# A graph network's edge sort and message stage: places from pairwise comparisons, halves of 9 and 9 edge tiles, seven target classes

## The chip, the cores and the metric

The kernel runs on one core of a Trainium2 chip, in one launch. The metric is device time in microseconds. An execution is timed as a whole; one further execution is recorded by the hardware profiler, and everything said about where the time goes comes from that one.

## What is computed

The graph has 3,125 nodes with 256 features and 50,000 edges with 16 features each. Sources are random; targets are drawn with a square law, and edges come ordered by target. One layer of message passing, then three graph convolutions over the same edges, each block behind a layer norm and a ReLU:

```python
h = jnp.maximum(_layernorm(x, axis=-1), 0.0)
# block 1
msg_input = jnp.concatenate([h[src], h[dst], edge_features], axis=-1)
messages = jax.nn.relu(msg_input @ mW1 + mb1) @ mW2 + mb2
aggregated = jax.ops.segment_sum(messages, src, num_segments=3125)
u = jax.nn.relu(jnp.concatenate([h, aggregated], -1) @ uW1 + ub1)
x = x + h + u @ uW2 + ub2
# block 2, three layers, gelu between them
h = jnp.maximum(_layernorm(x, axis=-1), 0.0)
# layer: y = h @ W; out = segment_sum(y[src] * dis[src] * dis[dst], dst) + b
x = x + gcn(gelu(gcn(gelu(gcn(h)))))
```

The hidden width is 512; `dis` is one over the root of a node's count of incoming edges, itself included.

## The kernel before

**Layout.** Node n belongs to node tile t = n mod 25, and its row in the tile is n div 25, so there are 25 node tiles (`NT`) of 125 rows (`NP`). The edges lie on chip as 128 partitions by 391 columns (`SCOLS`); a column is 128 edges.

**Stage 1, the sort (to about 565 us).** Each edge is given a place in a table in HBM, `rows_d`, sorted by the node tile of its source and, inside that, by a class of its target. There are two tables, for two halves of the edges: the first 240 columns (`SPLIT`) and the other 151. In the first a node tile has room for 11 edge tiles of 128 edges, in the second for 7 (`KT`). A row holds 20 numbers (features, target, row of the source in its tile, column of the target in the adjacency matrix).

The place of an edge is the number of edges of the same key before it. The key is 5 x source tile + target class, 125 values, one for each partition. `load_keys` broadcasts the keys of up to 24 columns from HBM (`bk_d`) to all partitions; `sort_chunk` (L330 to L392) compares them with the partition's number (L336, `eq`), runs a prefix sum over four columns at a time (L345, `cum`), adds what came before (`carry`, L351), keeps it where the key matches (L348, `q`), and lets a matmul with ones collapse the partitions to one place per edge (L354, `p_pos`). Some small VectorE steps turn places into row numbers (L358 to L376); ACT copies build the rows (`pay`, L386 to L389). In the first half each column is then scattered by an indirect DMA that GpSimd issues (L170, 128 rows of 80 bytes). The second half's rows wait on chip in `pay1` and `place1`. `fills` first writes empty rows to both tables.

Between the chunks of columns the program places other work, by position in the program: layer norm statistics (L151), h = relu(norm(x)) (`norm`), the tables `tabA` and `tabB` (L427), which hold h times the source's and the target's part of `mW1`, and the counting of incoming edges by one-hots (`count_edges`: ACT, L470 and L473, and a matmul, L475). The stores of these tables and of h transposed (`hT`, L422) go out on SyncE's queue (SP), which also issues the loads of edge features (`ea_st`) and of the broadcast keys.

**Stage 2, the messages (565 to 1850).** For each half q and node tile t, for each edge tile k of that node tile: GpSimd gathers the targets' rows of `tabB` (L725, `gb`, five buffers); PE makes the features' and the source's part (L730, L732, `p_x`); VectorE adds them (L733), ACT and VectorE make the ReLU in two pieces (L735, L736, `m`); PE sums over the edges of a source by a one-hot (L746, `p_sum`). Beside the edge tiles of one node tile run the adjacency counts of the one before: `counts` (L674) compares the targets' columns with an iota for a class of 626 columns (L681, `od`), once for each pair of class and edge tile that can meet (`REACH`), and PE multiplies it with the source's one-hot in two pieces of 313 columns (L683, `p_A`, one buffer of two banks); `counted` moves each class to the matrix A (L697 by ACT in the first half, L701 added by VectorE in the second). In the first half, the scatters of the second half's rows are put between the gathers, spread over the edge tiles of the first 24 node tiles. In the second half the node update (`nd`, L539 to L574) runs beside the edge tiles too, two node tiles late.

A test of the counts against `REACH` sets a flag, and a message stage that goes edge column by edge column stands behind it for inputs that do not fit.

**Stage 3, three graph layers (1850 to 2431).** PE multiplies A with the node products (L1004) in 7 blocks of 448 columns.

PE, VectorE (DVE), ScalarE (ACT), GpSimd (POOL) and SP each work through their instructions in program order. What stands ahead in an engine's or a queue's order holds up what is behind it.

## Time and profile before

| | us |
|---|---|
| median of three runs (2421.38 to 2439.94) | 2425.44 |
| the profiled execution | 2433.28 |
| its span, first to last instruction | 2431.6 |
| busy: PE, PEld, DVE, ACT, POOL | 1948.0, 1570.6, 1561.4, 1010.5, 858.9 |
| first scatter, last place computed, first edge tile | 72.5, 550, 565 |
| second half of the messages begins | 1275 |

Engines are named PE (TensorE matmul), PEld (weight load), DVE (VectorE), ACT (ScalarE), POOL (GpSimd), SP (SyncE). In a row of a group, the line and the engine come first, then what is written and read with the shapes (partitions x elements), the count, and after the bar the busy time in us and the mean time of one in ns; then the idle time of the engine just before these instructions and what ended most of it. The slices show busy time in tenths in forty equal parts of the span; PEclk is the granted clock of TensorE in tenths. A chain of waits is the work that ended last, followed back from its end; "issue" is time in which an engine waited for nothing that the profile shows, "remote" and "another core or an unknown queue" an event whose source the profile does not know.

### The profile page before, as it was taken

Reading aid. Unit: us, or ns where it says so; the run is one execution under the profiler, and the core shown is the slowest. Engines: PE = TensorE matmul, PEld = TensorE weight load, DVE = VectorE, ACT = ScalarE, POOL = GpSimd, SP = SyncE. Lnnn points to the kernel's source line nnn. Section 1 sums busy time; section 2 is a strip of 40 time slices with the busy share of each in tenths; the row PEclk is TensorE's granted clock in tenths of the full one; section 3 lists DMA queues with packets and bytes.
Section 4 is the critical chain, followed back from the end, with each engine's and each line's share of the span. In section 5 each row is a group of like instructions: output and inputs, shape, how many; then the busy total and the mean of one; then the engine's idle time right before and its main releaser. Section 6 shows DMA issues by size and latency. Waiting matters only on the chain.

```text
span 2431.6 us, 30795 instructions
## 1 busy us (share of the span) xinstructions
PE 1948.0 (80%) x10314; PEld 1570.6 (65%) x10314; DVE 1561.4 (64%) x3618; ACT 1010.5 (42%) x2070; POOL 858.9 (35%) x895
## 2 busy tenths in 40 slices
PE   3224554675888888888889999999996999999993
PEld 3223232354665666665667888888885898998992
DVE  4636343595877888887879999999983323223221
ACT  0415443452444545454444444444433544434440
POOL 0656656304666666666653332333210000000000
PEclk9999666776999899999989999999997999999995
DMA  7102343325544444444444444444432000000003
GB/s 223 43 6 82 101 148 86 101 102 160 152 135 135 130 140 140 136 140 131 136 135 143 142 142 136 144 141 142 142 86 77 22 1 1 1 1 1 1 1 107
DMA packets 117792, 242.64 MB, mean 100 GB/s; under 512 B 19790, under 2 KB 65348, under 8 KB 117491
## 3 DMA queue, kind: packets, MB, share of 16 engines
q0 software_dynamic: 48512, 122.02, 18.5%
q1 hardware_dynamic: 55996, 103.64, 13.2%
q10 hardware_dynamic: 13108, 14.84, 2.0%
q8 instruction: 85, 1.39, 0.2%
q14 instruction: 91, 0.75, 0.1%
HBM read 193.31 MB, written 47.12 MB: 99 GB/s over the span
## 4 chain that ended last, share of the span: by engine, by line
PE 58%; DVE 12%; issue 7%; another core or an unknown queue 7%; DMA 7%; ACT 5%; POOL 2%; ACTq 1%; SPq 0%; DVEq 0%; POOLq 0%
PE p_o L1004 17%; PE p_A L683 8%; PE p_sum L746 7%; PE p_x L732 7%; PE nd L563 4%; PE p_x L730 3%; DVE gb L733 3%; PE p_g L974 2%; DVE od L681 2%; DVE m L736 2%; PE p_tab L427 2%; PE tr L665 2%; DMA out<-xrow 2%; PE nd L572 2%
## 5 line engine op out<-in xcount | busy, mean ns | idle before, releaser
L725 POOL DMA_INDIRECT gb<-tabB,rows x450 | 454.6, 1010 | 590.0 <-DVE m L736 410.2
L170 POOL DMA_INDIRECT rows_d<-pay,place x391 | 398.1, 1018 | 254.1 <-issue 116.6
L1004 PE MATMUL p_o<-a,g 125*128 125x448 f32 x2100 | 443.1, 370 | 0.0
L1004 PEld LDWEIGHTS p_o<-a,g 125*128 125x128 f32 x2100 | 394.7, 188 | 32.4 <-ACT g L976 0.3
L746 PE MATMUL p_sum<-m,oh 128*125 128x512 f32 x900 | 389.5, 466 | 18.8 <-issue 8.2
L735 ACT ACTIVATE m<-gb 128x512 fp32r<-128x512 f32 x450 | 283.4, 634 | 227.8 <-DVE gb L733 161.3
L683 PE MATMUL p_A<-od,oh_h 128*125 128x313 f16 x1800 | 360.5, 305 | 21.3 <-ACT A L697 11.1
L733 DVE TENSOR_TENSOR gb<-gb,p_x 128x512 f32<-128x512 f32 x450 | 305.0, 678 | 81.3 <-remote 24.7
L732 PE MATMUL p_x<-apc,ohT 125*128 125x512 f32 x900 | 344.5, 430 | 8.9 <-ACT ohT L667 6.7
L736 DVE SCALAR_TENSOR_TENSOR m<-gb,m 128x512 fp32r<-128x512 f32 x450 | 306.4, 684 | 64.7 <-ACT m L735 43.4
L681 DVE TENSOR_SCALAR od<-iota_h,dloc 128x626 f16<-128x626 f16 x900 | 331.6, 397 | 7.9 <-PE p_A L683 6.4
L683 PEld LDWEIGHTS <-oh_h 128*125 128x125 f16 x1800 | 246.8, 140 | 95.4 <-issue 35.0
L998 DVE CAST a<-A 125x448 fp32r<-125x448 uint8 x262 | 102.8, 393 | 273.7 <-PE p_o L1004 273.5
L1000 ACT CAST a<-A 125x448 fp32r<-125x448 uint8 x263 | 148.7, 566 | 240.8 <-PE p_o L1004 240.8
L730 PE MATMUL p_x<-wE,payT 128*128 128x512 f32 x450 | 209.7, 466 | 25.4 <-DVE gb L733 20.7
L746 PEld LDWEIGHTS p_sum<-m,oh 128*125 128x125 f32 x900 | 172.7, 196 | 80.5 <-ACT m L735 17.6
L732 PEld LDWEIGHTS p_x<-apc,ohT 125*128 125x128 f32 x900 | 174.7, 198 | 32.8 <-ACT ohT L667 13.3
L427 PE MATMUL p_tab<-wAB,hT 128*125 128x512 f32 x200 | 126.7, 791 | 73.6 <-issue 46.2
L354 PE MATMUL p_pos<-ones_r,q 128*128 128x2 f32 x391 | 83.0, 323 | 72.4 <-DVE carry L351 40.4
L427 PEld LDWEIGHTS p_tab<-wAB,hT 128*125 128x125 f32 x200 | 48.6, 256 | 134.5 <-issue 104.7
L354 PEld LDWEIGHTS p_pos<-ones_r,q 128*128 128x128 f32 x391 | 72.8, 262 | 86.8 <-issue 42.4
L668 ACT CAST oh_h<-oh 128x375 f16<-128x375 f32 (+1 forms) x125 | 71.2, 569 | 135.8 <-DVE oh L659 121.6
(193 smaller groups left out, 2437.9 us busy)
## 6 DMA issues: line engine op xcount, KB each, us to landing
apc<-tabA SPq DMA_DIRECT2D x50, 500.0 KB
tabA<-a_sb SPq DMA_DIRECT2D x25, 500.0 KB
bk<-bk_d SPq DMA_DIRECT2D x16, 768.0 KB
gb<-tabB,rows POOLq DMA_INDIRECT x450
rows_d<-pay,place POOLq DMA_INDIRECT x391
tabB<-b_sb SPq DMA_DIRECT2D x25, 250.0 KB
R_d<-R SPq DMA_DIRECT2D x25, 250.0 KB
R<-R_d SPq DMA_DIRECT2D x25, 250.0 KB
```

Source lines behind the costliest of these rows:

```text
L170: s = nc.gpsimd.indirect_dma_start(out=rows_d[q], in_=pay, in_offset=None, out_offset=bass.IndirectOffsetOnAxis(ap=place, axis=0))
L427: nc.tensor.matmul(p, hT[:, k, :], wAB[:, s, k, :], start=k == 0, stop=k == 1)
L681: nc.vector.tensor_scalar(od, iota_h, dloc[q, t][:, g, k:k + 1], None, op0=ALU.is_equal)
L683: nc.tensor.matmul(p[:, h_, :HALF], oh_h[q, t][:, k, :], od[:, h_ * HALF:(h_ + 1) * HALF], start=k == lo, stop=k == hi)
L725: gathers[0] = nc.gpsimd.indirect_dma_start(out=gb, out_offset=None, in_=tabB, in_offset=bass.IndirectOffsetOnAxis(ap=row[q, t][:, k, C_DS ...
L730: nc.tensor.matmul(p, payT[q, t][:, k // 2, :], wE[k % 2], start=True, stop=False)
L732: nc.tensor.matmul(p, ohT, apc[q, t][:, s, :], start=False, stop=s == 1)
L733: nc.vector.tensor_add(gb, gb, p)
L735: nc.scalar.activation(m[:, 0, :], gb, AF.Relu)
L736: nc.vector.scalar_tensor_tensor(m[:, 1, :], gb, 0.0, m[:, 0, :].bitcast(F32), op0=ALU.max, op1=ALU.subtract)
L746: nc.tensor.matmul(p_sum[t], oh, m[:, s, :], start=k == 0 and s == 0, stop=k == KT[q] - 1 and s == 1)
L1004: nc.tensor.matmul(po[:, f, :AW], g[:, s, q, f * P:(f + 1) * P], a, start=s == 0 and q == 0, stop=s == NT - 1 and q == 1)
```

## The change

1. **Places.** The broadcast of keys through HBM, the prefix sums over one-hot keys and the carries go. For four columns at a time, `same_bucket` lets PE spread each column's keys over the partitions (a matmul of an identity column with the transposed keys), VectorE compares each edge's key with those of the other 127 of its column and keeps the earlier ones (`same`), and PE sums them. PE also turns the one-hots of the source tile (`eqT`), to look up for each edge how many edges of its key lie in earlier columns (`base`). These come from counts per column, made by one small matmul per column, and one prefix sum over 25 partitions by 7 classes by all columns of the half (`begin_places`).
2. **Halves and chunks.** 195 and 196 columns instead of 240 and 151; room for 9 and 9 edge tiles per node tile instead of 11 and 7. The chunks after which places are written are of 15 and five of 36 columns, then five of 36 and 16, instead of 24 each. `pay` has four buffers instead of three, `ea_st` three instead of two, `hT` three instead of two.
3. **Classes.** Seven target classes of 448 columns instead of five of 626. `od` is made once for an edge tile, over all classes that it can meet (one to four, 448 to 1,792 wide), instead of once for each pair. `p_A` is one bank with two buffers.
4. **Order.** Layer norm and tables run beside the first half's sort only, and all of the counting beside the second's. Of 25 blocks of counting one-hots, 16 are made by VectorE, one instruction a column, and 9 by ACT as before. Fills are four DMAs on SP instead of ten on ACT's queue. The load of x waits for the keys. What prepares the message stage (`wE`, `iota_h`, `first`) moves under the sort; the node weights load when the second message half begins, in `pay1`'s space.
5. Rows of A are now contiguous, so `col()` goes, and the graph layers' row of `dis` is one load.

```diff
-SPLIT = 240
-CH = 24
-KT = (11, 7)
-NG, GT = 5, 5
-REACH = (((0, 2), (1, 4), (3, 6), (5, 8), (6, 10)), ((0, 1), (0, 3), (1, 4), (3, 5), (4, 6)))
+SPLIT = 195
+CHUNKS = [15] + [36] * 5, [36] * 5 + [16]
+KT = (9, 9)
+NG, AW = 7, 448
+REACH = (((0, 1), (0, 2), (1, 4), (2, 5), (3, 6), (4, 7), (5, 8)),) * 2
+CLASSES = [[[g for g in range(NG) if r[g][0] <= k <= r[g][1]] for k in range(n)]
+           for r, n in zip(REACH, KT)]
...
+        def begin_places(q):
...
+            for b in range(NT):
+                nc.vector.tensor_scalar(eq_s[q][:, b, :n], cs_h[:, a:e], float(b), None,
+                                        op0=ALU.is_equal)
...
+                for c in range(m):
+                    nc.tensor.matmul(p[:NT, c * NG:(c + 1) * NG], eq_s[q][:, :, c0 + c - a],
+                                     eq_g[:, :, c0 + c], start=True, stop=True)
+                nc.scalar.copy(by_c[:, c0 - a:c0 - a + m, :],
+                               p[:NT, :m * NG].rearrange("t (c g) -> t c g", g=NG))
...
+            nc.vector.tensor_tensor_scan(cum, ones[:NT, 0:1].to_broadcast([NT, NG * n]), cnt, 0.0,
+                                         op0=ALU.mult, op1=ALU.add)
+            nc.vector.tensor_sub(base[q].rearrange("t g c -> t (g c)"), cum, cnt)
...
-            eq = g1.tile([P, P * CH], BF16, name="eq", bufs=2)
-            nc.vector.tensor_scalar(eq[:, :n], bk[j][:, :n], pid[:, 0:1], None, op0=ALU.is_equal)
...
-                nc.vector.tensor_tensor_scan(cum[:, :m], ones_p[:, 0:1].to_broadcast([P, m]),
-                                             eq[:, a], 0.0, op0=ALU.mult, op1=ALU.add)
...
-                    nc.tensor.matmul(pp[:, c, :], qq[:, c * P:(c + 1) * P], ones_r,
-                                     start=True, stop=True)
+        def same_bucket(q, c, n):
+
+            bc = gps.tile([P, R4, P], F32, name="bc", bufs=2)
+            for j in range(n):
+                i, r = divmod(c + j, P)
+                m = min(P, SCOLS - i * P)
+                nc.tensor.matmul(bc[:, j, :], ident_h[:m, r:r + 1].to_broadcast([m, P]),
+                                 bkT[:m, i, :], start=True, stop=True)
+            t = gps.tile([P, R4, P], F32, name="eqT_ps")
+            for j in range(n):
+                nc.tensor.matmul(t[:NT, j, :], eq_s[q][:, :, c + j - HALVES[q][0]], ident_h, start=True, stop=True)
+            same = g1.tile([P, R4, P], F16, name="same", bufs=3)
+            for j in range(n):
+                nc.vector.scalar_tensor_tensor(same[:, j, :], bc[:, j, :], bkey[:, c + j:c + j + 1],
+                                               tri, op0=ALU.is_equal, op1=ALU.mult)
+            eqT = g1.tile([NT, R4, P], F16, name="eqT", bufs=3)
+            nc.scalar.copy(eqT[:, :n, :], t[:NT, :n, :])
+            return same, eqT
...
+                for j in range(n):
+                    nc.tensor.matmul(pp[:, u + j:u + j + 1], same[:, j, :], ones_h, start=True,
+                                     stop=True)
+                    b = CW + (u + j) * NG
+                    nc.tensor.matmul(pp[:, b:b + NG], eqT[:, j, :],
+                                     base[q][:, :, c0 + u + j - HALVES[q][0]],
+                                     start=True, stop=True)
+                if u + n == w:
+                    placed(q, c0, w, pp)
+                if i >= behind:
+                    beside(i + 1 - behind, len(parts) - behind)
...
         def counts(q, t, g, k):
...
-            od = mp.tile([P, GS], F16, name="od", bufs=4)
-            nc.vector.tensor_scalar(od, iota_h, dloc[q, t][:, g, k:k + 1], None, op0=ALU.is_equal)
-            for h_ in range(2):
-                nc.tensor.matmul(p[:, h_, :HALF], oh_h[q, t][:, k, :],
-                                 od[:, h_ * HALF:(h_ + 1) * HALF],
-                                 start=k == lo, stop=k == hi)
+            if g == own[0]:
+                od = mp.tile([P, iota_h.shape[1]], F16, name="od", bufs=6)
+                n = len(own) * AW
+                nc.vector.tensor_scalar(od[:, :n], iota_h[:, :n], dloc[q, t][:, k:k + 1], None,
+                                        op0=ALU.is_equal)
+                targets[q, t, k] = od
+            b = (g - own[0]) * AW
+            nc.tensor.matmul(p_A[t], oh_h[q, t][:, k, :], targets[q, t, k][:, b:b + AW],
+                             start=k == lo, stop=k == hi)
```

`begin_places` runs once at the start of each half; `same_bucket` is called one group of four columns ahead of the matmuls that use it; `placed` ends a chunk with VectorE steps as before (two more, which pick the class), the row copies and, in the first half, the scatters.

## The prediction

> **What bounds the kernel now.** First the slices of the span, then the busy time by stage, to see which stage has an engine at its limit.
>
> ```profile
> PE 3224554675888888888889999999996999999993
> DVE  4636343595877888887879999999983323223221
> PEclk9999666776999899999989999999997999999995
> ```
>
> ```profile
> 70.00:250.00 180.00, 48.53 (x250) 41.06 (x250) 86.73 (x204) 61.27 (x170) 115.41 (x120) 0.97 0.17 46
> 250.00:450.00 200.00, 109.89 (x422) 60.63 (x422) 89.39 (x155) 80.91 (x214) 113.27 (x116) 0.69 0.38 110
> 450.00:568.00 118.00, 71.80 (x337) 48.82 (x338) 85.69 (x191) 56.91 (x146) 15.83 (x19) 0.69 0.35 113
> 568.00:1275.00 707.00, 600.88 (x2790) 437.43 (x2790) 560.55 (x1201) 341.57 (x617) 446.31 (x426) 0.92 0.48 138
> 1320.00:1820.00 500.00, 498.81 (x3247) 440.62 (x3246) 476.10 (x1209) 206.90 (x408) 145.87 (x154) 1.00 0.46 135
> ```
>
> Columns of the second view: the stretch, its length, busy PE, PEld, DVE, ACT, POOL, granted clock, DMA share, GB/s. Three stages read differently. The sort (to about 565) fills no engine: its busiest, DVE, is at 54% (the first 70 us add 35.6). The first half of the messages (568 to 1275) has PE at 85%, the second (to 1820) PE at 100%. The rest, three graph layers, is PE at 100% and is not touched.
>
> Then the chains of waits of the sort (70 to 560) and of the second message half (1320 to 1820):
>
> ```profile
> by line: another core or an unknown queue 22.5%; issue 19.4%; PE p_tab L427 10.1%; POOL rows_d L170 8.1%; DVE cum L345 7.3%; ACT off L470 5.9%; DMA rows_d<-pay,place 4.8%; DVE q L348 4.7%; ACT oh L473 2.9%; DMA tabB<-b_sb 2.7%; DMA rows<-ro
> ```
>
> ```profile
> by line: PE p_A L683 19.5%; PE nd L563 16.4%; PE p_sum L746 15.3%; PE p_x L732 14.5%; PE nd L550 8.4%; PE nd L572 8.0%; PE p_x L730 7.3%; PE tr L665 3.4%; PE nd L552 2.1%; PE nd L539 2.0%; PE tr L651 1.8%; DVE od L681 0.3%; DVE m L736 0.3%;
> ```
>
> In the sort 41.9% of 490 us, 205 us, is on no engine. The timeline shows a part of it: instructions that wait for nothing start 1.40 us apart while POOL scatters.
>
> ```profile
> 132.44 0.27 DVE L462 TENSOR_SCALAR eq_c<-cs_b 128x391 bf16<-128x391 bf16 x1 [1.07 <-issue]
> 132.88 0.96 POOL L170 DMA_INDIRECT rows_d<-pay,place  x1 [0.30 <-issue]
> 133.84 0.27 DVE L462 TENSOR_SCALAR eq_c<-cs_b 128x391 bf16<-128x391 bf16 x1 [1.13 <-issue]
> ```
>
> Another part is queueing on SP: loads of features and of broadcast keys wait there for buffers, ahead of the tables' stores (hT waits 89.9 us for "remote", ten times). Last the groups that give prices:
>
> ```profile
> L170 POOL DMA_INDIRECT rows_d<-pay,place x391 | 398.1, 1018 | 254.1 <-issue 116.6 <-DVE carry L351 93.3 <-ACT pay L389 19.7
> L681 DVE TENSOR_SCALAR od<-iota_h,dloc 128x626 f16<-128x626 f16 x900 | 331.6, 397 | 7.9 <-PE p_A L683 6.4 <-PE tr L665 1.3
> L345 DVE TENSOR_TENSOR_SCAN cum<-ones_p,eq 128x512 f32<-128x512 f32 x97 | 115.6, 1217 | 6.5 <-remote 4.4 <-issue 1.3 <-DVE cum L345 0.8
> L348 DVE SCALAR_TENSOR_TENSOR q<-cum,carry,eq 128x512 fp32r<-128x512 f32 x97 | 71.5, 737 | 15.6 <-remote 10.9 <-issue 3.0 <-DVE ln_st L151 0.9
> L354 PE MATMUL p_pos<-ones_r,q 128*128 128x2 f32 x391 | 83.0, 323 | 72.4 <-DVE carry L351 40.4 <-DVE q L348 14.5 <-DVE b_sb L436 7.1
> L336 DVE TENSOR_SCALAR eq<-bk,pid 128x3072 bf16<-128x3072 bf16 x16 | 16.2, 1012 | 5.9 <-DMA bk<-bk_d 5.9
> ```
>
> **Sort, what leaves and what comes.** DVE loses scan, q, carry (14.1) and eq: 115.6+71.5+14.1+16.2 = 217 us. It gains 391 comparisons of 128 wide. No row has them: the same operation takes 0.17 us at 24 elements (L360), 0.616 at 384 and 0.737 at 512, so 0.30 by the line between the first two and 0.37 by that between the last two; since successors start some 0.08 us before an end, 0.23 is the low end. I take 0.25, nearer to the short form: 98 us (90 to 145). Place computations are 12 x 11 steps of some 0.2 us for 16 x 8 of 0.1 (now 0.16 to 0.18, overlapped): 13 more; counting one-hots moved from ACT are 256 x 0.10 = 26 (391 wide back to back is 0.174), two scans of 1,365 elements at 1,217/512 ns each 6.5. DVE falls from 297 to about 224.
>
> The Trainium skill ("VectorE: DVE Perf Modes", on the fixed extra latency of each SBUF-source instruction) speaks against many narrow instructions: one wide tile pays the fixed part once, small ones each time. Its formula (N+151)/0.96 gives 290 ns at 128, against 712 at 512 where the row has 737; the comparisons would then be an estimated 114 us, not 98, and the sort 16 us longer at most.
>
> PE loses 83 us (L354) and gains per column two 128-column f16 matmuls, two small ones, and a count that replaces one as large. An f16 matmul of 313 columns takes 0.133 us in the second message half, L475's with 25 columns 0.11 to 0.12 at low clock: 0.10 and 0.07, so 0.34 x 391 = 133 (95 to 200). PE to 568 goes from 259 to 309 and is now the busiest. ACT gains 98 copies of about 0.6 and loses 16 of 25 blocks of L470 and L473 (158 us in all): 42 less. The 17 broadcasts of keys leave SP (12.5 MB). Feature loads get a third buffer, so they no longer hold back the stores there; the fills (four, from 10) go to SP too, behind the first loads and ahead of nothing that is wanted before 70 us. The x load now waits in ACT's queue for the keys (landed at 22.7 us); behind it stand ACT's key copies, which need them anyhow, and DVE's comparison of keys stands behind the first normalisation statistics, which need x.
>
> **Sort, the path.** Scatters run 1.26 us apart (0.96+0.30). The first started at 72.5; x landed at 31.8 and will be later, but no keys go through memory: I keep 70 (60 to 80). POOL then sends 15, waits in its queue (a memset of the next pay, behind ACT's copies) to about 100, and the other 180 take 228: done at 328, which ends nothing but its own rows. ACT's copy of the sixth payload waits for the 36 scatters of the second to land, about 150; layer norm, table copies and eqT copies stand behind it. From there 25 tables at 5.2 us (chain pieces 3.5 at full clock, 7.3 at worst) = 130, beside 21 parts of four columns at 4 x 0.34 = 1.4: 29. The first half ends near 310. The second has no scatters and DVE work of 49+7+26+13+8 = 103; at 0.73, DVE's share in 450 to 568, 141 us: 451. The first edge tile follows in 14 (before, 548 to 565; its preparation moves under the sort): 465, **100 us earlier**. Ends: 400, if PE or DVE keep over 90% in the second half; 565 below.
>
> **Messages, first half (9 tiles for 11).** From the chain of the second half, 22.9 node tiles in 500 us: p_A 19.5% = 4.25 us per node tile, 0.133 each of 32; node update 36.9% = 8.05; the rest 42.3%, 1.32 per edge tile. At full clock before: 11 x 1.32 + 40 x 0.133 = 19.8; after, with 25 matmuls of 448 columns (0.190 each): 9 x 1.32 + 4.75 = 16.6. Measured 28.3, so by PE 28.3 x 16.6/19.8 = 23.7. DVE per node tile, busy 22.4: two edge tiles less, 2.7; `od` from 20 x 0.397 = 7.9 to nine of 448 to 1,792 wide, 9 x 0.24 + 11,200 x 0.25 ns = 5.0 (slope from 626 at 397 to 3,072 at 1,012): about 17. POOL has 17.04 instructions per node tile now (426 in 25) and 9 + 196/24 = 17.2 after: 21.6 us, so it goes from 76% to 91% of the period. That close, I add 0.6: 24.3 x 25 = 608, **99 less** (555 at POOL's pace and little else; 665 at 26.6).
>
> **Messages, second half (9 for 7).** 8.05 + 4.75 + 9 x 1.32 = 24.7 against 21.8: **+72**. It has no slack, PE is at 100%; DVE comes to about 23.5, hidden under it, and would add up to 12 if it led. Node weights (about 2 MB on SP) now load in this half's first node tile, behind the same scatters as its rows; first used two node tiles on, free, 14 us uncovered. p_A's second buffer saves PE 11.1 us of waits (L697), inside the 608. The graph layers keep their 7 blocks, and one load replaces five: 0.
>
> **Sum.** 2433.3 (span 2431.6 and 1.7 around it) - 100 - 99 + 72 = 2306. The profiled run stands 7.8 over the median: **2298**.
>
> **Rivals.**
> - *Gain lost in the sort.* It keeps the old efficiency, busiest engine 54%, so it ends at 309/0.54 = 572, 22 later. For it: the 205 us on no engine are unexplained. Against it: the second half has no scatters and SP lost its queue. Then 2433 + 22 - 27 - 8 = 2420, from 2385 to 2440.
> - *More gain.* The sort ends at 400 (-151) and the first message half runs at POOL's pace (-152): 2433 - 151 - 152 + 72 - 8 = 2194, from 2150 to 2225. Against it: that stage has held 70% of PE's full-clock pace (19.8 of 28.3).
> - *Slower: loss per instruction.* The 205 us belong to the 2,686 instructions of PE, DVE and ACT to 568, 76 ns each. The change makes about 4,350 of them (PE 2,650): 332 us lost, where the rest falls only by some 12 us of work, so the first edge tile comes at about 680: 2433 + 115 - 27 - 8 = 2513. It decides from 56 ns each, where a loss of 244 eats both gains (205 + 27 + 12). For it: the 1.40 us grid holds whatever the instruction is. Against it: the longest of these waits end with SP's stores, which no count explains.
>
> What the Trainium skill says of instruction fetch ("Runtime: NRT & Kernel Launch", Instruction fetch mechanics) counts against the last one: refills come ahead of use and are hidden by the issue rate. By it the loss would not grow with their number; this trace shows 85 and 91 refill packets but not who waited for them.
>
> That the counts exceed a class's reach, so that edges go column by column, is excluded: counted from the inputs, every range holds.
>
> **How the numbers follow.** Forecast (first edge tile at 430 to 520, messages within 40 of their sum): 2225 to 2385, 0.62. More gain 0.14. Gain lost 0.13, most of it within 1% of 2425 (2401 to 2450, about what can be told from no change). Slower 0.11. The range 2190 to 2430 leaves out slower and half of more gain. Faster 0.62 + 0.14 + 0.05 = 0.81, same 0.08, slower 0.11.
>
> **What would show it.** PE and DVE over 70% in the last 130 us before the first gather; that gather at 440 to 490; "issue" and "unknown" under 150 us in the sort's chain; node tiles 24 and 24.7 us apart; POOL over 85% of its pace in the first. Wrong if the sort's second half takes over 200 us, or gathers come to bound PE.

## The result, and the profile after

The changed kernel takes 2515.24 us (median of 4 runs, 2513.37 to 2517.27), the one before 2432.69 (4 runs, 2421.38 to 2440.48). The ratio is 1.0343 [1.0291, 1.0395]: **slower**, where 2298 and faster had been forecast. The profiled execution has a span of 2515.5 us against 2431.6. Cut at the first and the last sum of edge messages (`p_sum`) and at the second half's first gather, the span falls into these stages:

| us | before | after | measured | forecast |
|---|---|---|---|---|
| to the first `p_sum` (sort) | 576.3 | 638.6 | +62 | -100 |
| first message half | 692.9 | 648.8 | -44 | -99 |
| second message half | 545.9 | 624.1 | +78 | +72 |
| the rest | 616.5 | 604.1 | -12 | 0 |

First the slices of the span of the kernel after; each digit is the busy share of a fortieth of it, in tenths, in the last row the granted clock.

```profile
PE   3435546698677787787799999999997999999993
DVE  4323323466566676676689999999995323323221
POOL 1554354100666666666643333333330000000000
PEclk9999678655789898898999999999998999999995
```

The first ten slices, the sort, look no denser than before, and DVE is emptier. Then the busy time by stage (stretch, its length, busy PE, PEld, DVE, ACT, POOL, granted clock, DMA share, GB/s):

```profile
70.00:250.00 180.00, 79.14 (x487) 52.24 (x486) 56.51 (x201) 38.26 (x94) 93.33 (x100) 0.99 0.14 35
250.00:450.00 200.00, 102.05 (x473) 54.73 (x472) 64.57 (x222) 32.73 (x73) 92.91 (x96) 0.74 0.32 91
490.00:617.00 127.00, 120.18 (x989) 97.02 (x987) 87.39 (x393) 50.05 (x107) 0.00 (x0) 0.50 0.01 4
640.00:1285.00 645.00, 492.98 (x2037) 344.99 (x2036) 432.26 (x805) 296.26 (x597) 428.32 (x410) 0.88 0.45 130
1310.00:1900.00 590.00, 588.39 (x3448) 485.68 (x3446) 556.41 (x1304) 263.25 (x543) 208.63 (x215) 1.00 0.49 144
```

Two things stand out. From 70 to 450 PE is busy 48% and DVE 32%: the first half of the sort lasts until about 490 instead of 310. And the second half, 127 us long, has PE at 95% at a granted clock of 0.50. The chain of waits gives no pieces for 65 to 635 of this kernel, so the timeline has to show where the first half's time goes. ACT's row, then PE's, while 36 scatters run from 99 to 144 (start, duration, and in brackets the idle time before and what ended it):

```profile
113.31 0.57 ACT L341 CAST eqT<-eqT_ps 25x512 f16<-25x512 f32 x1 [7.97 <-remote]
139.99 0.57 ACT L341 CAST eqT<-eqT_ps 25x512 f16<-25x512 f32 x1 [26.11 <-remote]
```

```profile
113.93 0.59 PE L335 MATMUL eqT_ps<-ident_h,eq_s 128*25 128x128 f16 x4 [6.34 <-issue]
...
116.61 0.19 PE L409 MATMUL p_pos<-base,eqT 25*128 25x7 f16 x1
140.62 0.58 PE L335 MATMUL eqT_ps<-ident_h,eq_s 128*25 128x128 f16 x4 [23.82 <-issue]
```

The input of ACT's second copy was written by PE at 114.5; the copy starts at 140.0, and PE stands from 116.8 to 140.6. Summed from the instruction records up to the last place, stretches of over 1 us in which PE, ACT and DVE all stand (called the standstill below) make 169 us of the sort here and 114 us before, nearly all of them while scatters are being issued one after the other. Of these, 156 us here and 66 before end with a wait that the profile puts down to "remote", as in ACT's two rows. The groups that the forecast priced:

```profile
L338 DVE SCALAR_TENSOR_TENSOR same<-bc,bkey,tri 128x128 f16<-128x128 f32 x391 | 115.2, 342 | 184.3 <-remote 109.9 <-PE bc L331 59.5 <-PE p_tab L459 7.9
L406 PE MATMUL p_pos<-ones_h,same 128*128 128x1 f16 x391 | 72.9, 187 | 3.3 <-issue 2.8 <-DVE same L338 0.6
L409 PE MATMUL p_pos<-base,eqT 25*128 25x7 f16 x391 | 72.3, 185 | 6.8 <-DVE base L310 6.8
L335 PE MATMUL eqT_ps<-ident_h,eq_s 128*25 128x128 f16 x391 | 61.4, 292 | 69.3 <-issue 50.1 <-ACT eqT L341 18.6
```

The comparisons cost 115.2 us, and the 109.9 us of "remote" ahead of them are the same standstill seen from DVE.

### The profile page after: what moved, and what is told of

Read it like the earlier page. It is cut to its first block, busy times and chain, and to the rows that moved or that the text cites. A ratio compares the mean times of both kernels' runs of the same rounds, so it can differ in the third digit from the quotient of the medians.

```text
span 2515.5 us, 32086 instructions
## 1 busy us (share of the span) xinstructions
PE 2038.5 (81%) x10936; PEld 1598.1 (64%) x10936; DVE 1477.8 (59%) x3673; ACT 979.0 (39%) x2012; POOL 855.7 (34%) x907
## 5 line engine op out<-in xcount | busy, mean ns | idle before, releaser
L724 PE MATMUL p_A<-od,oh_h 128*125 128x448 f16 x1250 | 381.8, 366 | 37.0 <-issue 20.6
L770 PE MATMUL p_x<-apc,ohT 125*128 125x512 f32 x900 | 353.4, 456 | 40.7 <-ACT ohT L702 24.8
L720 DVE TENSOR_SCALAR od<-iota_h,dloc 128x1344 f16<-128x1344 f16 (+3 forms) x450 | 245.3, 561 | 0.1
L770 PEld LDWEIGHTS p_x<-apc,ohT 125*128 125x128 f32 x900 | 182.4, 203 | 94.0 <-issue 33.4
L768 PE MATMUL p_x<-wE,payT 128*128 128x512 f32 x450 | 219.6, 488 | 11.8 <-DVE gb L771 7.4
L338 DVE SCALAR_TENSOR_TENSOR same<-bc,bkey,tri 128x128 f16<-128x128 f32 x391 | 115.2, 342 | 184.3 <-remote 109.9
L724 PEld LDWEIGHTS <-oh_h 128*125 128x125 f16 x1250 | 173.5, 141 | 75.5 <-issue 23.8
L459 PE MATMUL p_tab<-wAB,hT 128*125 128x512 f32 x200 | 112.7, 716 | 70.4 <-ACT hT L449 63.1
L735 ACT CAST A<-p_A 125x448 uint8<-125x448 f32 x175 | 93.1, 532 | 169.1 <-PE p_A L724 72.5
L341 ACT CAST eqT<-eqT_ps 25x512 f16<-25x512 f32 x98 | 56.2, 573 | 168.3 <-remote 76.4
```

The costliest lines, as they stand in the source:

```text
L459: nc.tensor.matmul(p, hTs[c][:, k, :], wAB[:, s, k, :], start=k == 0, stop=k == 1)
L720: nc.vector.tensor_scalar(od[:, :n], iota_h[:, :n], dloc[q, t][:, k:k + 1], None, op0=ALU.is_equal)
L724: nc.tensor.matmul(p_A[t], oh_h[q, t][:, k, :], targets[q, t, k][:, b:b + AW], start=k == lo, stop=k == hi)
L768: nc.tensor.matmul(p, payT[q, t][:, k // 2, :], wE[k % 2], start=True, stop=False)
L770: nc.tensor.matmul(p, ohT, apc[q, t][:, s, :], start=False, stop=s == 1)
```

## The experiments

The theories: **streams**, an unbroken run of scatters holds up the hand-offs between the other engines (the standstill above); **count**, the rival "loss per instruction"; **clock**, PE at half clock sets the sort's second half; and for the first message half, that GpSimd's extra scatters delay the gathers. The runs come in five groups, and the kernel before is in each. It took 2443, 2390, 2268, 2266 and 2266 us in them, the first and the last on the same chip, for a reason that these runs don't show; so kernels are compared inside a group, and a comparison across groups is called one.

**First group (before: 2443.06).** `e1_no_scatter0`, the change without the first half's scatters:

```diff
-            if q == 0:
-                for c in range(w):
-                    scatter(0, place[:, c:c + 1], pay[:, c, :])
```

> Leaves out the 195 scatters of the first half's rows (its edges are missing from the output); all else is as in the changed kernel. Streams theory (while GpSimd issues scatters back to back, the other engines hardly get on; PE, ACT and DVE are all idle for 169 us between 60 and 640, nearly all of it inside the five streams): that idle time falls under 40 us, the first half of the sort ends 110 to 150 us earlier (near 320 instead of 460), and the total falls by as much, to 2365 to 2405. Loss-per-instruction theory (the rival on record that came out near the measured time): PE, ACT and DVE issue the same instructions, so the idle time stays over 140 us and the total within 25 us of 2515.

2356.71 us. The first gather comes at 459 and the first `p_sum` at 471, the standstill falls to 23 us, the tables end at 313 and the second half's last comparison at 451. The window that held 36 scatters, and the second half:

```profile
99.00:144.00 45.00, 41.27 (x226) 25.63 (x225) 28.02 (x95) 18.30 (x36) 0.00 (x0) 0.92 0.21 68
335.00:451.00 116.00, 114.24 (x916) 91.33 (x915) 81.15 (x379) 44.78 (x92) 0.00 (x0) 0.50 0.00 1
```

The same 45 us with all 36 scatters, in the fourth kernel of this group, e4:

```profile
99.00:144.00 45.00, 8.14 (x64) 6.40 (x64) 6.73 (x28) 2.78 (x6) 34.26 (x36) 1.00 0.07 11
```

Without them PE does five times the work. (Until a trace's first record of the clock, at 215 us in e4 and at 120 in e1, it counts as 1.00, so the 1.00 here is no reading.) Count falls here: the three engines issue as many instructions as before.

`e2_paced` keeps the scatters and puts a GpSimd fill (`iota` of 1,000 columns, 0.99 us) behind each:

```diff
                 for c in range(w):
                     scatter(0, place[:, c:c + 1], pay[:, c, :])
+                    pause(1000)
```

> Puts an iota of 1,000 columns on GpSimd after each scatter of the first half, so that scatters start some 2.4 us apart instead of 1.26; nothing is left out. Streams theory: with GpSimd not issuing back to back, PE, ACT and DVE idle together under 70 us instead of 169 and the first half ends near 360 instead of 460, although the scatters themselves take longer (195 x 2.4 = 468 us from 65, so to about 535, under the second half's sort); first edge tile 550 to 600 instead of 638, total 2425 to 2480. If instead the number of scatters counts and not their spacing, the idle time stays at 169 or grows, and the total is 2515 to 2560. Loss per instruction: no change in the idle time, total near 2515.

2396.98 us. The first `p_sum` comes at 512, against 629 in e4 and 681 in e3 below (42 of them its added matmuls), which scatter unpaced, and the standstill is 21 us. The same window:

```profile
99.00:144.00 45.00, 42.34 (x249) 27.54 (x249) 29.57 (x96) 19.01 (x38) 41.23 (x42) 0.96 0.22 62
```

GpSimd is 92% busy and the others work. So neither GpSimd's load nor the number of scatters makes the standstill here: the closeness of the scatters does. One thing more differs in e2. ACT's copy of the sixth payload has to wait until the second chunk's scatters have landed, since there are four payload buffers; it is about the 290th instruction in ACT's order in e2 and about the 114th in the kernel after. It doesn't explain the 169 us, for in the trace of the first result no standstill ends with that copy; in the fourth group it counts.

`e3_filler4` adds four matmuls of 512 columns to each group of the second half's sort, to lift the clock:

```diff
+            if q == 1:
+                for _ in range(4):
+                    nc.tensor.matmul(t.rearrange("p a b -> p (a b)"), ident_h,
+                                     eq_s[q].rearrange("p t c -> p (t c)")[:, :H],
+                                     start=True, stop=True)
```

> Adds four matmuls of 512 columns (f16, 128x128 weights, result thrown away) to each of the 49 groups of four columns of the second half's sort, which runs 127 us from 490 to 617 at a granted clock of 0.50 with PE 98% busy. Clock theory (small matmuls do not count as activity, so the clock stays halved; more streaming lifts it): the clock there rises over 0.9, a group takes 2.6/2 + 4 x 0.22 = 2.2 us instead of 2.6, and the total falls by 10 to 25 us. If the low clock has another cause: 49 groups x 4 x 0.43 = 84 us longer, total near 2600.

2563.05 us. The second half's groups take 169 us (489 to 658), some 42 more than the 127 above, neither the gain nor the full loss expected. Its windows:

```profile
490.00:550.00 60.00, 59.46 (x518) 38.77 (x517) 37.91 (x172) 24.32 (x54) 0.00 (x0) 0.90 0.00 1
550.00:660.00 110.00, 108.28 (x706) 68.58 (x705) 58.67 (x305) 38.62 (x86) 0.00 (x0) 0.56 0.00 1
```

The clock rose to 0.90 for 60 us and fell back with the fillers still there. Whether the half clock can be lifted cheaply stays open.

`e4_no_scatter1` leaves out the second half's 196 scatters, which run between the first message half's gathers:

```diff
-                        scatter(1, place1[:, late_done:late_done + 1], pay1[:, late_done, :],
-                                gathers[0])
```

> Leaves out the 196 scatters of the second half's rows, which stand between the gathers of the first message half (its edges are missing from the output). First message half now 667 us, 26.7 per node tile, against 24.3 forecast. If GpSimd's place in the queue and its bursts cause the surplus: 540 to 590 us, total 2435 to 2460 less nothing elsewhere. If PE, DVE and ACT by themselves set it (16.6 us of PE at full clock at the old 70%): 640 to 667, total within 25 us of 2515.

2335.58 us. The first message half takes 468.6 us, against 651 to 657 in the other three of this group and 649 in the first result: 0.92 to 0.96 us for each scatter. Its window:

```profile
630.00:1095.00 465.00, 445.12 (x2039) 308.91 (x2037) 426.32 (x807) 297.12 (x596) 217.22 (x219) 0.99 0.58 175
```

PE is at 96%, so 18.7 us per node tile is near PE's own pace; the forecast's sum at full clock was 16.6.

**Second group (before: 2390.28).** Is it GpSimd's time or the scatter itself that delays the gathers? `e5_iota_for_scatter1` puts fills of about the same length in the scatters' place; `e6_q0_paused` puts a short one ahead of each scatter:

```diff
-                        scatter(1, place1[:, late_done:late_done + 1], pay1[:, late_done, :],
-                                gathers[0])
+                        pause((512, 512, 200))
```

> As the changed kernel, but each of the 196 scatters of the second half's rows, between the gathers of the first message half, is replaced by GpSimd iotas of 512, 512 and 200 columns (about 1.3 us, as long as a scatter with its gap; those rows are then missing). Without the scatters that half took 468 us, with them 649. If GpSimd's time is what the scatters cost (gathers come later): 600 to 650 us here. If it is the scatter as a DMA, or its closeness to other indirect DMAs, and not GpSimd's time: 470 to 510 us.

```diff
+                        i = pause((300,))
+                        scatter(1, place1[:, late_done:late_done + 1], pay1[:, late_done, :], i)
```

> As the changed kernel, with an iota of 300 columns (about 0.35 us) on GpSimd ahead of each scatter between the gathers of the first message half. If indirect DMAs issued back to back hold up the other engines there as in the sort, the pauses break the bursts: that half falls from 649 to 560 to 620 us, total 2430 to 2490. If GpSimd's time sets the pace: 196 x 0.35 = 69 us more, 690 to 720, total 2555 to 2590. If each scatter has a price of its own whatever its spacing: 640 to 660, total near 2515.

With fills alone (2491.04 us) the half takes 613.7 us, GpSimd busy 526 of them, against 469 with nothing in their place (e4, another group): most of the price is the place that each takes in GpSimd's queue ahead of a gather. With pauses (2492.85) it takes 623.2; no unpaused twin ran in this group, so this one decides nothing.

`e7_before_no_scatter1` leaves out the 151 scatters among the gathers of the kernel **before** (the same edit as in e4), and `e8_before_paced` puts a fill of 400 columns behind each of its 240 scatters in the sort:

```diff
+    def pause(lag, width):
+        i = nc.gpsimd.iota(lag[:, :width], pattern=[[1, width]], base=0, channel_multiplier=0)
...
+                    pause(cell["lag"], PW1)
```

> The kernel before, without its 151 scatters between the gathers of the first message half (those rows are then missing). In the changed kernel 196 scatters cost 181 us there, 0.92 each. If the price is per scatter, this half falls from 693 (first sum to the second half's first gather) by 139 to about 555, and the total by as much; then the surplus of the old half over PE's full-clock 495 was scatters, and scaling it by PE's work, as the prediction did, was the error. If the old half was slow for its 11 edge tiles and shapes: it stays over 640.

> The kernel before, with an iota of 400 columns (about 0.45 us) on GpSimd after each of the 240 scatters of its first half, so that they start some 1.72 us apart. If back-to-back scatters held up its sort too (PE, ACT and DVE all idle 114 us there): idle time under 50, first edge tile 480 to 530 instead of 565, total 2385 to 2420 beside 2443 (or 2425). If its sort has another limit (keys from memory, the chain of scans): within 12 us of the kernel before.

e7 takes 2307.64 us, its first message half 568.9 against 681.2 in e8, where nothing was changed in that half: the old kernel's 151 scatters cost 0.74 us each here. e8 takes 2352.5, its sort 507.8 against 572.7 in e7: the kernel before pays for its streams too, and pacing gets part of it back. But e8's standstill is 63 us (e7: 99), not the under 50 expected, and of another kind: none of it ends with "remote", and 51 us end with ACT's copies of payloads, which wait for scatters to land.

**Third group (before: 2267.69).** What of a scatter does it? `e9_gather_for_scatter0` turns each first-half scatter into a gather of the same rows, `e10_iota_for_scatter0` into a fill of 1,240 columns:

```diff
-                    scatter(0, place[:, c:c + 1], pay[:, c, :])
+                    s = nc.gpsimd.indirect_dma_start(
+                        out=pay[:, c, :], out_offset=None, in_=rows_d[0][:n_rows[0], :],
+                        in_offset=bass.IndirectOffsetOnAxis(ap=place[:, c:c + 1], axis=0))
```

> As the changed kernel, but each of the 195 scatters of the first half is turned round: an indirect DMA of the same 128 rows of 80 bytes from the table into the payload's place on chip, back to back as before (those edges' rows stay empty). With the scatters PE, ACT and DVE were all idle 169 us before the first edge tile, without them 23. If any stream of indirect DMAs issued back to back holds the engines up: idle over 120 again, first edge tile 600 to 640. If it is the writing to HBM: idle under 50, first edge tile 465 to 500, total 2350 to 2390.

```diff
-                    scatter(0, place[:, c:c + 1], pay[:, c, :])
+                    i = nc.gpsimd.iota(lag[0][:, :1240], pattern=[[1, 1240]], base=0,
+                                       channel_multiplier=0)
```

> As the changed kernel, but each of the 195 scatters of the first half is replaced by a GpSimd iota of 1,240 columns (about 1.25 us), behind the same places and payloads (those rows are missing). If GpSimd being busy is enough to hold the others up: idle over 120, first edge tile 600 to 640. If it takes indirect DMAs: idle under 50, first edge tile 465 to 490, total 2345 to 2380.

First `p_sum` at 501.9 (standstill 43 us) and 476.2 (22). No unpaced kernel of the change ran in this group, and in the next one, where the kernel before takes as long, it has 522 and 58; so the times leave the gather between the two. The trace of e9 says more: its longest standstill, 21.6 us, ends when ACT's copy of the sixth payload, at 137.3, has its buffer, and so does that of e13 below. `e11_before_no_scatter0` leaves out the 240 scatters of the kernel before, and `e12_after_both` is the change with a pause of 600 behind the sort's scatters and one of 300 ahead of the others:

```diff
-                for c in range(w):
-                    scatter(0, place[:, c:c + 1], pay[:, c, :])
+                pass
```

> The kernel before without the 240 scatters of its first half (their rows are missing). Gives the old way of finding places without the stalls, to set beside 471 us to the first sum in the changed kernel without its scatters. If the new places are the gain that was forecast (100 us, of which the fewer scatters are a part): the first sum comes at 520 to 570. If the old sort too was slow through its scatter streams alone (114 us of idle time): 450 to 480, and the new places save nothing.

```diff
+                    pause(600)
...
+                        i = slow((300,))
+                        scatter(1, place1[:, late_done:late_done + 1], pay1[:, late_done, :], i)
```

> The changed kernel with an iota of 600 columns after each scatter of the first half (period about 1.9 us) and one of 300 ahead of each scatter in the first message half; nothing is left out. Streams theory: first sum at 485 to 515 instead of 638, first message half 623 instead of 649, total 2350 to 2380, 0.965 to 0.985 of the kernel before. Loss per instruction: near 2515, 1.03 to 1.05.

e11: 2181.77 us, first `p_sum` at 405.7, standstill 9; DVE is busy 292 of the 394 us to the first gather, 74%. e12: 2359.43, ratio 1.0419 [1.0361, 1.0476]. Its time and its first `p_sum` (508.6) are as expected, but the ratio is a miss, since the kernel before takes 2268 here.

**Fourth group (before: 2265.66): both kernels, with and without all scatters.** `e13_after_again` and `e14_before_again` are unchanged, `e15_after_none` has the edits of e1 and e4, `e16_before_none` those of e7 and e11.

> The changed kernel again, unaltered, on one chip with the next three. By its first result 1.03 to 1.04 of the kernel before, with the first sum about 62 us later, the first message half 44 us shorter, the second 78 longer and the rest 11 shorter. If the first result depended on its chip, these differ: on the chip where the kernel before took 2268, the first message half with scatters took 580 and not 650 in two variants, so up to 70 us less there.

> The kernel before again, unaltered, for its profile on the same chip: its stages are what the other three are set against.

> The changed kernel without any scatter (all edges' rows are missing). From runs on other chips: first sum at 471, first message half 468, second 625 to 632, total about 2175. The difference to the changed kernel on this chip is the whole price of its 391 scatters.

> The kernel before without any scatter (all edges' rows are missing). From runs on other chips: first sum at 406, first message half 569, second 547, total about 2140. If that holds on one chip, the change loses 30 to 40 us with no scatter in it at all (sort 65 longer, first half 101 shorter, second 80 longer, rest 11 shorter), and the rest of its loss is the 45 scatters that moved from the sort to the gathers. If the old sort without scatters took 460 or more here, the new places would be level, and scatters the whole loss.

| us | before (e14) | after (e13) | change | before, no scatters (e16) | after, no scatters (e15) | change |
|---|---|---|---|---|---|---|
| to the first `p_sum` | 501.0 | 522.4 | +21 | 406.7 | 484.4 | +78 |
| first message half | 606.9 | 582.2 | -25 | 583.0 | 491.1 | -92 |
| second message half | 546.1 | 624.1 | +78 | 547.7 | 633.5 | +86 |
| the rest | 615.2 | 606.2 | -9 | 617.9 | 605.8 | -12 |
| span | 2269.2 | 2334.9 | +66 | 2155.3 | 2214.8 | +60 |
| standstill in the sort | 74 | 58 | | 8.5 | 27 | |

e13 has three rounds: ratio 1.0272 [1.0217, 1.0326]. The change is slower with scatters and without; scatters cost the old kernel 114 us and the new one 120, so they don't make the difference. They cost it in different places, 94 us in the sort and 24 in the first message half of the old kernel, 38 and 91 in the new one.

The standstill shows another cause here than in the first group. None of it ends with "remote" in any kernel of the last three groups. In e14 55 of the 74 us end with ACT's copies of payloads, which wait until earlier scatters have landed and their buffer (one of three) is free, and so does the longest stretch of e13, 22 us from 115.5, with the copies of `eqT` behind it in ACT's order. Two rows of e14, then that of e13:

```profile
136.01 0.51 ACT L386 COPY pay<-ea_st 128x384 f32<-128x384 f32 x1 [13.77 <-DMA rows_d<-pay,place]
166.31 0.51 ACT L386 COPY pay<-ea_st 128x384 f32<-128x384 f32 x1 [28.28 <-DMA rows_d<-pay,place]
```

```profile
137.50 0.67 ACT L381 COPY pay<-ea_st 128x576 f32<-128x576 f32 x1 [24.46 <-DMA rows_d<-pay,place]
```

Whether more payload buffers would help either kernel was not tried.

What makes the difference is in the sort without scatters. The old one, to 390, then the new one, to 465:

```profile
70.00:250.00 180.00, 121.82 (x549) 81.46 (x550) 144.00 (x304) 123.49 (x339) 0.43 (x3) 0.91 0.35 119
250.00:390.00 140.00, 96.11 (x459) 63.95 (x457) 113.17 (x243) 73.02 (x190) 0.95 (x3) 0.74 0.35 127
```

```profile
70.00:250.00 180.00, 144.04 (x789) 87.32 (x788) 97.89 (x320) 55.32 (x133) 0.11 (x1) 0.87 0.27 87
250.00:350.00 100.00, 80.71 (x566) 51.25 (x565) 48.59 (x200) 40.56 (x98) 0.00 (x0) 0.78 0.33 106
350.00:465.00 115.00, 113.28 (x906) 90.59 (x905) 80.35 (x376) 43.69 (x89) 0.00 (x0) 0.50 0.00 1
```

The old sort keeps DVE at 80% and PE at 68%, tables and both halves side by side. The new one keeps PE at 80%, then at 98% of a half clock, with DVE at 70% and no table left to make beside it: the change took work off DVE and set it on PE where PE is slowest. In the first message half (e14, then e13):

```profile
501.00:1108.00 607.00, 559.08 (x2729) 404.56 (x2728) 548.50 (x1176) 331.97 (x604) 447.30 (x420) 0.98 0.54 157
```

```profile
522.00:1105.00 583.00, 487.92 (x2057) 334.16 (x2056) 432.71 (x816) 301.24 (x602) 445.79 (x414) 0.92 0.49 145
```

PE and DVE lose 71 and 116 us of work and the stage loses 25: what was a stage of PE and DVE now waits for gathers, with POOL at 76%. VectorE's addition to the gathered rows shows it (time waited, times, longest), in e14 and in e13:

```profile
DVE gb L733 <- DMA gb<-tabB,rows: 41.2, 26, 4.0
```

```profile
DVE gb L771 <- DMA gb<-tabB,rows: 114.2, 59, 4.9
```

**Fifth group (before: 2266.40, five rounds).** Does a part of the change pay alone? `e17_before_od` is the kernel before with one `od` for up to two classes, `e18_before_od_paced` that and the pauses of e8:

```diff
+            own = [v for v in range(NG) if REACH[q][v][0] <= k <= REACH[q][v][1]]
+            own = own[own.index(g) // 2 * 2:][:2]
+            if g == own[0]:
+                od = mp.tile([P, 2 * GS], F16, name="od", bufs=4)
+                n = len(own) * GS
+                nc.vector.tensor_scalar(od[:, :n], iota_h[:, :n], dloc[q, t][:, g, k:k + 1], None,
+                                        op0=ALU.is_equal)
```

> The kernel before with one part of the change: target one-hots made once per edge tile for up to two of its classes (626 or 1,252 wide) instead of once for each pair; sort, halves and classes as before. If VectorE sets the first message half (22.4 us busy of 28.3 per node tile; 20 instructions become 12, some 2 us less), that half gets 30 to 50 us shorter and nothing else moves: 0.978 to 0.988 of the kernel before. If PE or GpSimd's scatters set it: 0.995 to 1.005.

> The same with an iota of 400 columns after each scatter of the sort (period about 1.72 us). On a chip where the kernel before takes over 2380, the first sum comes 40 to 70 us earlier than in the kernel before: 0.955 to 0.975. On one where it takes about 2268, the scatters end at about 490 by their pace alone, and it is level with the one without pauses or up to 10 us slower.

2266.46 us, ratio 1.0009 [0.9986, 1.0032], and 2269.58, ratio 1.0019 [1.0003, 1.0034]. In e17 DVE is busy 525 of 601 us in the first message half, in e14 549 of 607, and nothing follows: a gain of one to two per cent had been expected, and DVE was not what that stage waits for. Pauses that gave 1.6% in one run of the second group give nothing here; in e18 49 of the 59 us of standstill end with payload copies that wait for the scatters, which now come later. No version with all its edges was shown to beat the kernel before.

## Why the prediction was wrong

**The step that failed is "Sort, the path".** It set a path for the new sort, 465 us, against a measured 565 of the old one, and took the whole difference for the gain. But the 565 held what scatters cost the old sort: without them it is at its first gather by 394 and at its first `p_sum` by 406 (e11, e16). So by its engines' own work the change makes the sort 78 us *longer* (e15 against e16; across groups, by e1's 471, 65). The new sort pays for scatters as well: in the first group 158 us (e4 against e1); for the old one, 576 in the first result against 406 in later groups, an estimate across groups, would be 170. Thus +62 in place of -100. In the fourth group, where both run with scatters and without, it is 94 for the old and 38 for the new, and +21.

That e1 meets the path's times (310 for the first half's end, 451 for the second's, 465 for the first edge tile; e1 has 313, 451 and a first gather at 459) is partly luck. The term "25 tables at 5.2 us = 130" was mis-sized: in e1 the tables run from 113 to 313, 8 us each, but they start at 113 and not at 150, since no scatter is waited for. With scatters, in e13, they start at 144, nearly as forecast, and end at 363.

The 205 us on no engine were also read wrongly where they were read. The prediction put the waits of `hT` down to SP's queue. The ten that end with "remote" wait for PE's semaphore alone, and the same copies in the same kernel hardly wait in e14. The kernel before in the first result, then in e14:

```profile
L422 ACT COPY hT<-p_tab 128x250 f32<-128x250 f32 x25 | 9.1, 364 | 96.9 <-remote 89.9 <-PE p_tab L419 5.8 <-issue 1.1
```

```profile
L422 ACT COPY hT<-p_tab 128x250 f32<-128x250 f32 x25 | 9.0, 362 | 14.4 <-PE p_tab L419 12.2 <-DMA hT_d<-hT 2.1
```

The rest of the 205 us the prediction called unexplained, used for its rivals, and let the forecast drop.

Why the own work grows: to the first gather of e1 DVE is busy 265 us (224 forecast) and PE 363 (309 forecast). L406 and L409 take 187 and 185 ns each and overlap in part, and the clock is 0.50 for the whole second half. "At 0.73, DVE's share" gave the right length of that half for the wrong engine: DVE is busy 69% of it, PE 95%. And the tables, beside the first half alone, are paced by their stores; without scatters the last one comes at 333 in the old kernel and at 327 in the new one (e16, e15), but the new one has its whole second half still to do. The chain of waits of e1 from 65 to 460 is made up of the following (line numbers from 403 on are three lower than in the kernel after):

```profile
by line: DMA tabA<-a_sb 37.6%; PE eqT_ps L335 10.5%; PE p_pos L406 8.0%; PE p_small L543 6.8%; PE p_pos L403 6.7%; PE p_tab L456 5.9%; PE bc L331 5.7%; ACT eqT L341 4.1%; PE p_tab L303 2.5%; DMA rows<-rows_d 1.9%; DVE a_sb L460 1.8%; issue 
```

So neither half could take up the other's slack.

**First message half, -99 forecast, -44 measured.** The scaling by 16.6/19.8 was right where nothing else bounds: -92 without scatters. The term "+0.6" for POOL was the one mis-sized: the half takes 26.0 us per node tile, 2.3 over the 23.7 by PE. Forty-five more scatters run among the gathers, and each costs more than it did in the old kernel: 0.92 to 0.96 us (e4) against 0.74 (e8 and e7, another group), and in the fourth group 0.46 (e13 against e15: 91 us in 196) against 0.16 (e14 against e16: 24 us in 151). That the gathers hide less because PE's period is shorter is an argument; no run changes the one without the other. Counted as the prediction counts, 1.26 us for each of its instructions, POOL fills 80 to 90% of the half (410 in 645 us, 414 in 583 us in e13), near the 91% it gave; its busy share reads only 66 to 76%, so a GpSimd that looks a quarter idle can already be what a stage waits for.

**Second message half, +72, measured +78:** right, with PE at 100% in both. **`od`:** 5.0 us per node tile forecast, 245.3/50 = 4.9 measured; right, and worth nothing by itself (e17). **`same`:** 98 us forecast, 115.2 measured, 295 ns each. The formula of the Trainium skill's "VectorE: DVE Perf Modes" (on the fixed extra latency), which that page gives for the addition of two fp32 tensors, had given 290 ns and an estimated 114 us, and was the better price; at 512 elements it gives 691 ns, not the 712 of the prediction, where the row has 737. **The rest:** -12 was not forecast; 10 of it lie between the last `p_sum` and the graph layers' first `p_o` (52 us before, 42 after), and which of the edits does it was not tried.

**The rivals.** "Loss per instruction" gave 2513, the measured 2515, with the wrong cause: e1 and e2 issue as many instructions on PE, ACT and DVE and lose 21 to 23 us, not 169. The Trainium skill ("Runtime: NRT & Kernel Launch", Instruction fetch mechanics) had spoken against it, and here the runs agree. "Gain lost in the sort" named the right mechanism, stalls that stay, and gave 572 to the end of the sort; with PE's true 363 us its own rule would give 363/0.54 = 672, against 618. Of "what would show it", the second half's density came true (PE 95%, DVE 69%), and nearly the pace of the second message half (25.0 us per node tile); the first gather at 626 spoke against the forecast as it was meant to, and gathers did come to bound the first message half.

**Open:** what the dense scatters block where waits end with "remote", and why the same kernel took 2443 us in one group and 2266 in another, with the standstill 114 us in the first trace and 74 in the later one. One difference stands in the traces. Those of the later three groups hold 16 records of landing for each of GpSimd's DMAs, those of the first two only 6 to 11, and 14 to 16 in e2's sort, which has no such waits. Where hand-offs came late, records are missing too, so the recording itself may have a part in it; this was not tried, nor were scatters into memory on the chip. The step from dense streams to late hand-offs is shown for the first group (e1, e2); in the fifth, spacing the scatters bought nothing.

## What to carry to other kernels

Before a stage is credited with what a model of its engines gives, run the kernel as it is with the suspected wait taken out: a stall-free model of the new must be set against a stall-free run of the old, never against its measured time. Work that moves off a half-idle VectorE onto many small matmuls is priced at the clock that such matmuls get. Indirect DMAs that share GpSimd's queue with gathers are counted by their place in that queue, not by GpSimd's busy share. And a copy that waits for its buffer holds up all that stands behind it in its engine's order.

## What the runs showed of the hardware

- In the first result and the first group, scatters of 128 rows issued 1.26 us apart went with late hand-offs among the other engines: a copy whose input was ready at 114.5 started at 140.0, and 156 of 169 us of standstill ended so. With a fill of 0.99 us behind each scatter (e2) none did, and 21 us were left; in the last three groups none did either, at the same 1.26 us.
- The granted clock stayed at 0.50 for 115 to 127 us in which PE was 95 to 98% busy with matmuls of 1 to 128 columns (e1, e15 and the kernel after). Matmuls of 128 columns start 0.106 us apart there, and 0.056 in e3's stretch at 0.90 (medians). The Trainium skill ("TensorE: Matmul & The Clock Gate", What's actually happening) lets a busy window of some microseconds open the gate; this trace differs, and four matmuls of 512 columns per group (e3) opened it for 60 us alone.
